# A GNN chain on one Trainium2 core: two norms without eigenvector pieces, the branch moved, three half blocks in the lead

## The chip, the cores and the metric

The kernel runs as one program on one core of a Trainium2 chip. Its time is the device time of one execution in microseconds (us). The engines are called as in the profile: PE (matmul, with PEld for its weight loads), DVE (vector), ACT (scalar), POOL (GpSimd) and SP, which here only issues DMAs. Each engine runs its own list of instructions in the order in which it was built; semaphores hold an instruction back until others have ended.

## What is computed

Four graph layers, each followed by `x = layernorm(x + layer(x))`, on x of 128 x 64 x 256 float32. The change touches layer 1, what leads from it into layer 2, and the eigenvectors of layer 3, which are worked out early, in pieces between other work.

```python
# layer 1: two matmuls, each with a norm over all 8192 rows
agg = jnp.einsum('nm,bmd->bnd', A_hat, features)
x = agg.reshape(-1, d)
h = jax.nn.relu(_batchnorm(x @ W1.T + b1, g1, be1))
out = h @ W2.T + b2
out = _batchnorm(out, g2, be2)
# layer 2, its edge scores:
e = jnp.einsum('behd,hd->beh', jax.nn.leaky_relu(Qs + Kt, 0.2), a)
# layer 3:
_, U = jnp.linalg.eigh(L_norm)
```

A batchnorm needs mean and variance of all rows before the first row can be scaled: at each of the two there is one point through which all work passes.

## The kernel before, in words

The 8192 rows are 64 tiles of 128 rows (`X`, kept on chip), taken four at a time as 16 blocks q (`NQ`).

**First pass** (loop at L1733). For each q, PE multiplies by the adjacency matrix (L1739) and by W1 (L1745, into `ps`); DVE takes the statistics of each result (`bn_stats` into `st1`, L1746); ACT copies it away (L1747). `pump(n)` puts about n us of eigenvector pieces, small DVE instructions and a few small matmuls, into the program at that place. `affine("n1", ...)` (L1709) turns the statistics into scale and shift: one `bn_aggr` for each of four groups (L1712), then a chain of small DVE steps with one square root on ACT (L1214), down to `n1sh` (L1722).

**Second pass** (loop at L1755). For each q ACT makes four pieces of `h` (L1758, in the order 2, 3, 0, 1), SP reloads X (L1759), PE multiplies by W2 (L1763, in the order 0, 1, 2, 3), DVE takes statistics (L1764) and copies the result to `Y` (L1765). `affine("n2", ...)` follows.

**The branch** (L1815). The fast eigenvector method leaves a flag `bad`; a general path stands behind a loop that runs 0 or 1 times by the value `again` (L1811). Every engine loads that value (TENSOR_LOAD), compares, jumps over the loop's body, and waits at the loop's exit until all engines have come there and all their earlier work has ended. The body has some 5,800 DVE instructions.

**Last pass** (`last_pass`, L1770) in 32 half blocks of two tiles. For half block h: ACT scales `Y` into `y` (L1778), PE transposes it (L1787), DVE adds it to X (L1234) and takes layernorm statistics (L1237, L1238). Every second half block `flush` works out the scale of four tiles: a DVE step (L1212), a square root on ACT (L1214), five DVE steps (L1215 to L1218, L1249), and ACT scales each tile (L1253). Each half block is two steps of a generator: transposes and add, then the rest.

**Scores of layer 2** (`scores`, L1910) run beside it, in 32 steps k of two tiles. A step transposes two normalised tiles (L1890, copied by DVE at L1892), maps them with a weight matrix (L1901; ACT copies at L1903 and L1904), and for c = 0 and 1 spreads them over edges (L1924, "l"), copies the result (ACT, L1931, four instructions), applies the leaky ReLU (DVE, L1932, four) and reduces with the vector a (PE, L1878). Four half blocks of the last pass come first; then every step k takes two more with it. The first l of a round waits for all four copies of the round before.

A scheduler places each instruction in its engine's list; the order in the source isn't the order in the list, except where `tc.issue_after` or `tc.keep_in_program_order` hold it.

Of the kernel before, what the change touches and what calls it, by code (L numbers as in the profile page):

```python
# [1 line left out]

# [5 lines left out]
F32 = mybir.dt.float32  # L8
I32 = mybir.dt.int32
AF = mybir.ActivationFunctionType  # L10
ALU = mybir.AluOpType
# [3 lines left out]
N = 64  # L15
# [1244 lines left out]
def tile_adj_resnorm(ctx: ExitStack, tc: tile.TileContext, I: dict, out: bass.AP, layers: int = 4):  # L1260
# [74 lines left out]
    def psum(rows, w):  # L1335
        return eps.tile([P, 512], F32, tag="eps", name="eps")[:rows, :w]
# [46 lines left out]
    def pump(n):  # L1383

        owed[0] += n
        body = nc.cur_bb.bb.instructions
        for i in reversed(body[seen[0] :]):
            if i.engine == mark[0].engine:
                mark[0] = i
                break  # L1390
        with tc.issue_after(mark[0]):
            while owed[0] > 0:
                owed[0] -= next(pieces, None) or 2.6
        seen[0] = len(body)
# [293 lines left out]
    own2 = lambda where, **k: own1(where, side="right", **k)  # L1688
    dram = keep1.enter_context(tc.tile_pool(name="l1d", bufs=1, space=bass.MemoryType.DRAM))
    lw, sm = own2(only1, name="l1w", bufs=1), own2(only1, name="l1s", bufs=2)  # L1690
    pp = own1(only1, name="l1p", bufs=7, space=PSUM)

    def lload(name, shape, src, eng=nc.sync):
        t = lw.tile(shape, F32, tag=name, name=name)
        eng.dma_start(t, src)
        return t

    NQ = NT // 4
    Y = [ly.tile([P, 2, 512], F32, tag=f"Y{q}", name="Y") for q in range(NQ)]
    w1 = lload("w1", [P, 2, 512], kio(I["W1T"]))  # L1700
    w2 = lload("w2", [P, 4, D], kio(I["W2T"]))
    vec1 = lload("vec1", [P, 3, 4], I["vec1"], s)
    vec2 = lload("vec2", [P, 3, 2], I["vec2"], s)
# [21 lines left out]
    def xq(q):  # L1725
        return X[:, q * 4 : q * 4 + 4, :]
# [5 lines left out]
    back = residual(NT // TG - 1, H, pp, "ps")  # L1732
    for q in range(NQ):  # L1733
        nc.sync.dma_start(xd[q], xq(q))
        at = sm.tile([P, 2, 512], F32, tag="at", name="at")
        for k in range(2):
            ps = pp.tile([P, 512], F32, tag="ps", name="ps")
            for j in range(4):
                te.matmul(ps[:, j * P : (j + 1) * P], X[:, q * 4 + j, k * P : (k + 1) * P], bdah,  # L1739
                          start=True, stop=True)  # L1740
            s.copy(at[:, k, :], ps)  # L1741
        for c in range(4):
            ps = pp.tile([P, 512], F32, tag="ps", name="ps")
            for k in range(2):
                te.matmul(ps, w1[:, k, c * P : (c + 1) * P], at[:, k, :], start=(k == 0), stop=(k == 1))  # L1745
            v.bn_stats(st1[:, c, q, :], ps)  # L1746
            s.copy(first(q, c), ps)  # L1747
        next(back, None)
        pump(4.5 if q < 8 else 6)
    zero = sm.tile([P, 1024], F32, tag="at", name="zero")  # L1750
    v.memset(zero, 0.0)
    for z in attn_d[: N * N, :].rearrange("(k p a) q -> k p (a q)", p=P, a=4):
        nc.sync.dma_start(z, zero)
    sc1, sh1 = affine("n1", st1, vec1, 4)
    for q in range(NQ):  # L1755
        h = sm.tile([P, 4, 512], F32, tag="h", name="h")
        for c in (2, 3, 0, 1):
            s.activation(h[:, c, :], first(q, c), AF.Relu, bias=sh1[:, c : c + 1], scale=sc1[:, c : c + 1])  # L1758
        nc.sync.dma_start(xq(q), xd[q])  # L1759
        for c in range(2):  # L1760
            ps = pp.tile([P, 512], F32, tag="ps", name="ps")
            for k in range(4):
                te.matmul(ps, w2[:, k, c * P : (c + 1) * P], h[:, k, :], start=(k == 0), stop=(k == 3))  # L1763
            v.bn_stats(st2[:, c, q, :], ps)  # L1764
            v.tensor_copy(Y[q][:, c, :], ps)  # L1765
        pump(5)
    sc2, sh2 = affine("n2", st2, vec2, 2)
    for _ in pieces:
        pass

    def last_pass():

        ln = Norm(nc, sy, X, 8, act=True)

        def normed(h):
            y = sy.tile([P, 2, 2 * P], F32, tag="y", name="y")
            for c in range(2):
                s.activation(y[:, c, :], Y[h // 2][:, c, h % 2 * 2 * P : (h % 2 + 1) * 2 * P], AF.Identity,  # L1778
                             bias=sh2[:, c : c + 1], scale=sc2[:, c : c + 1])
            return y  # L1780

        y = normed(0)
        for h in range(2 * NQ):
            ps = pp.tile([P, 512], F32, tag="m", name="m")
            for i in range(2):
                for c in range(2):
                    te.transpose(ps[:, i * D + c * P : i * D + (c + 1) * P], y[:, c, i * P : (i + 1) * P], ident)  # L1787
            ln.add(2 * h, ps, 2)
            yield
            if h % 2:  # L1790
                ln.flush()
            if h < 2 * NQ - 1:
                y = normed(h + 1)
            yield

    only1.close()
    beyond.close()
    own.close()


    def spread():
        for bd, m in ((bdu, U), (bdut, UT)):
            for b in range(2):
                r = slice(b * N, (b + 1) * N)
                v.tensor_copy(bd[r, r], m[r, :])

    with tc.tile_pool(name="eps3", bufs=1, space=PSUM) as eps:
        again = ek.tile([1, 1], I32, tag="again", name="again")
        ps = psum(1, 1)
        te.matmul(ps, fast.bad, ones[:N, 0:1], start=True, stop=True)  # L1810
        v.tensor_scalar(again, ps, 0.0, None, ALU.is_gt)  # L1811
        for bd in (bdu, bdut):
            v.memset(bd, 0.0)
        spread()
        with tc.For_i(0, nc.values_load(again[0:1, 0:1], min_val=0, max_val=1)):  # L1815
            with tc.tile_pool(name="gk2", bufs=1) as gk2, tc.tile_pool(name="gt2", bufs=1) as gt2, tc.tile_pool(
                name="gp2", bufs=1, space=PSUM
            ) as gp2:
                Eigh(tc, gk2, gt2, gp2, cst, ident, ones).from_leaves(*fast.state, U, UT)
            spread()  # L1820

    sy = own1(keep1, name="l1z", bufs=3)

# [3 lines left out]
    with ExitStack() as l2:  # L1827
# [67 lines left out]
        def maps(k, xT):  # L1895

            xq, xv = [], sx.tile([P, 2, D], F32, tag="xv", name="xv")
            for i in range(2):
                ps = pp.tile([P, 512], F32, tag="m", name="m")
                for c in range(2):  # L1900
                    te.matmul(ps, xT[:, i, c, :], wqv[:, c, :], start=(c == 0), stop=(c == 1))  # L1901
                xq.append(sx.tile([P, D], F32, tag="xq", name="xq", bufs=4))
                taken.append(s.copy(xq[i], ps[:, :D]))  # L1903
                s.copy(xv[:, i, :], ps[:, D:])  # L1904
            nc.sync.dma_start(xvd[k], xv)
            return xq

        def scores():


            K = NT // 2
            xT = transposed(0)
            xq, xT = maps(0, xT), transposed(1)


            four = [(b, i) for i in range(2) for b in range(2)]
            for k in range(K):
                xn = None
                for c in range(2):
                    xs, pl = {}, [pg.tile([P, 2, 512], F32, tag="l", name="l") for _ in range(2)]  # L1920
                    mms = []
                    for b, i in four:
                        r = slice(b * N, (b + 1) * N)
                        mms.append(te.matmul(pl[i][:, b, :], xq[i][r, c * P : (c + 1) * P], GG[r, :], start=True, stop=True))  # L1924
                    after(mms[0], taken)
                    del taken[:]
                    next(beside[0], None)
                    ready = []
                    for b, i in four:
                        x = xs[b, i] = sx.tile([P, E], F32, tag="xs", name="xs", bufs=6)  # L1930
                        taken.append(s.copy(x, pl[i][:, b, :]))  # L1931
                        ready.append(v.scalar_tensor_tensor(x, x, 0.2, x, ALU.mult, ALU.max))  # L1932
                    if late:
                        after(products(), mms[-1:], mybir.DependencyClass.NoSync)
                    late.append((k, c, xs, ready))
                    if c == 0 and k < K - 1:
                        xn = maps(k + 1, xT)
                    if c == 1 and k < K - 2:
                        xT = transposed(k + 2)
                    next(beside[0], None)  # L1940
                xq = xn
                if k == K - 1:
                    products()
                yield
# [91 lines left out]

        bank = None
        sc_, beside[0] = scores(), last_pass()
        run(*beside * 8)
        run(*[sc_] * (NQ - 2))  # L2040
        keep1.close()
        beside[0] = iter(())
        lw, sm = own1(valuing, name="l2w", bufs=1), own1(valuing, name="l2s", bufs=2)
        ln = Norm(nc, sm, X, 4, act=True)
        val = values()
        soft += [softmax(h, es[h]) for h in range(2)]
        run(*[sc_] * (HU - NQ + 2))
        for _ in range(3):
            run(sc_, soft[0], soft[0])
        run(soft[0], sc_)  # L2050
# [156 lines left out]
```

## Time and profile before

| | us |
|---|---|
| median of three runs | 2411.7 (2410.27 to 2413.79) |
| the profiled execution | 2413.07, span 2411.2 |

Busy time of PE by stretch of the span (a query over windows of the trace):

| stretch, us | what runs | PE busy | of |
|---|---|---|---|
| 1530 to 1570 | first pass | 39.83 | 40.00 |
| 1667 to 1676 | first norm | 2.09 | 9.00 |
| 1700 to 1740 | second pass | 40.00 | 40.00 |
| 1790 to 1803 | second norm, branch, first half blocks | 4.54 | 13.00 |
| 1803 to 1830 | half blocks, first scores | 22.16 | 27.00 |
| 1830 to 1900 | scores beside the last pass | 69.14 | 70.00 |

In lines of the timeline the columns are: start in us, length in us, engine, source line, operation, output<-input, shape, number of instructions merged, and in brackets how long the engine sat idle before, and what ended that. Lengths of PE matmuls are modelled; starts are measured.

### The profile page before, as it was taken

The page shows a single profiled execution, that of the slowest core. Times are in us where ns is not written, and L with a number is a line of the kernel's source. Part 1 is how long each engine was busy: PE and PEld are TensorE (multiplying, and loading weights), DVE is VectorE, ACT ScalarE, POOL GpSimd, SP SyncE. Part 2 cuts the span into 40 slices and gives each one's busy share as a digit, 9 for nine tenths or more (in the row PEclk, how much of TensorE's full clock was granted, in tenths as well). Part 3 has the DMA queues.
Part 4 walks back from the last instruction along what each step waited for, and adds up shares of the span by engine and source line. Part 5 has one row for each costly group of instructions (what it writes and reads, how often), then busy time and mean ns, then how long its engine had stood idle before and what let it go on. Part 6 is the DMA issues. An engine that isn't in the chain of part 4 may idle for free. (4 is left out here: it accounts for less than half of the span.)

```text
span 2411.2 us, 29498 instructions
## 1 busy us (share of the span) xinstructions
PE 2289.0 (95%) x9016; PEld 1226.7 (51%) x9016; DVE 1815.5 (75%) x8352; ACT 974.3 (40%) x1750; POOL 76.4 (3%) x115
## 2 busy tenths in 40 slices
PE   7999999999999999999999999998979999898897
PEld 5544654444565544665444644554434433246786
DVE  4666766677887888888888888686967877457577
ACT  2333322242333243332243322333437875456575
POOL 0000000000000000000000000000000000002231
PEclk9999999999999999999999999999989999999899
DMA  6001000000100010100001000012211000511622
GB/s 218 18 18 36 1 35 1 24 30 18 53 1 35 2 52 18 53 35 1 35 36 36 17 18 18 18 49 92 75 45 40 23 23 29 94 40 44 136 89 75
DMA packets 59861, 101.26 MB, mean 42 GB/s; under 512 B 5136, under 2 KB 40080, under 8 KB 59440
## 3 DMA queue, kind: packets, MB, share of 16 engines
q1 hardware_dynamic: 54624, 88.83, 11.6%
q0 software_dynamic: 3216, 10.21, 1.5%
q8 instruction: 72, 1.18, 0.2%
q14 instruction: 93, 0.76, 0.1%
q10 hardware_dynamic: 1856, 0.28, 0.1%
HBM read 67.84 MB, written 31.46 MB: 41 GB/s over the span
## 5 line engine op out<-in xcount | busy, mean ns | idle before, releaser
L1590 PE MATMUL pq<-H,wi 128*128 128x512 f32 (+1 forms) x2016 | 836.4, 547 | 6.1 <-DVE H L1619 4.0
L1596 ACT ACTIVATE gate<-pq,bl 128x512 f32<-128x512 f32 (+1 forms) x504 | 317.6, 635 | 791.0 <-PE pq L1594 642.3
L1590 PEld LDWEIGHTS pq<-H,wi 128*128 128x128 f32 x2016 | 371.9, 191 | 331.0 <-issue 256.7
L1594 PE MATMUL pq<-lh,wh 128*128 128x512 f32 (+1 forms) x1152 | 481.8, 534 | 16.0 <-DVE lh L1614 12.7
L1594 PEld LDWEIGHTS pq<-lh,wh 128*128 128x128 f32 x1152 | 213.1, 190 | 213.3 <-issue 128.3
L1932 DVE SCALAR_TENSOR_TENSOR xs<-xs 128x512 f32<-128x512 f32 x256 | 165.3, 682 | 63.6 <-ACT xs L1931 62.5
L1931 ACT COPY xs<-l 128x512 f32<-128x512 f32 x256 | 136.8, 587 | 74.8 <-PE l L1924 38.6
L1924 PE MATMUL l<-edge_s,xq 64*128 64x512 f32 x512 | 136.0, 629 | 17.5 <-ACT xs L1931 12.5
L1612 ACT ACTIVATE gate<-lc 128x512 f32<-128x512 f32 (+1 forms) x144 | 83.5, 580 | 166.6 <-DVE lc L1608 80.9
L1901 PE MATMUL m<-wqv,xT 128*128 128x512 f32 x256 | 123.0, 617 | 0.8 <-DVE xT L1892 0.8
L1763 PE MATMUL ps<-h,w 128*128 128x512 f32 x256 | 114.9, 608 | 6.9 <-ACT h L1758 6.9
L1745 PE MATMUL ps<-at,w 128*128 128x512 f32 x256 | 116.7, 607 | 3.8 <-ACT at L1741 3.2
L1253 ACT ACTIVATE X<-X,ln_sh,ln_rs 128x256 f32<-128x256 f32 x192 | 99.2, 590 | 19.5 <-DVE ln_sh L1249 13.7
L1237 DVE BATCH_NORM_STATS2 ln_st<-X 128x6 f32<-128x256 f32 x256 | 98.7, 415 | 2.3
L142 DVE COPY AQR<-eps 64x192 f32<-64x192 f32 (+1 forms) x125 | 35.0, 280 | 80.9 <-PE eps L148 80.8
L1901 PEld LDWEIGHTS m<-wqv,xT 128*128 128x128 f32 x256 | 46.0, 192 | 77.1 <-issue 62.5
L1763 PEld LDWEIGHTS ps<-h,w 128*128 128x128 f32 x256 | 49.1, 194 | 67.4 <-issue 57.5
L1924 PEld LDWEIGHTS l<-edge_s,xq 64*128 64x128 f32 x512 | 46.3, 189 | 69.8 <-issue 32.9
L1996 POOL DMA_DIRECT2D xr<-xv x32 | 17.6, 550 | 2007.2 <-DVE xs L1932 1791.2
L1610 DVE TENSOR_TENSOR gate<-gate 128x512 f32<-128x512 f32 (+1 forms) x72 | 43.4, 603 | 45.9 <-ACT gate L1596 45.3
L1745 PEld LDWEIGHTS ps<-at,w 128*128 128x128 f32 x256 | 47.2, 192 | 59.7 <-issue 46.8
L1878 PE MATMUL sc<-xs,az 128*32 128x512 f32 x512 | 68.2, 605 | 3.0 <-DVE xs L1932 3.0
(557 smaller groups left out, 3245.6 us busy)
## 6 DMA issues: line engine op xcount, KB each, us to landing
wi<-in_WihT_dram SPq DMA_DIRECT2D x16, 1024.0 KB, 4.9
wh<-in_WhhT_dram SPq DMA_DIRECT2D x12, 1024.0 KB, 6.9
X<-in_x_dram SPq DMA_DIRECT2D x16, 512.0 KB, 8.9
xd<-X SPq DMA_DIRECT2D x16, 512.0 KB, 2.7
X<-xd SPq DMA_DIRECT2D x16, 512.0 KB, 3.2
xv<-xv SPq DMA_DIRECT2D x32, 256.0 KB, 2.0
xr<-xv POOLq DMA_DIRECT2D x32, 256.0 KB, 3.0
M<-attn_d SPq DMA_DIRECT2D x16, 512.0 KB, 11.2
```

What stands on the lines that cost most here:

```text
L1237: nc.vector.bn_stats(st, self.X[:, k, :])
L1253: nc.scalar.activation(x, x, AF.Identity, bias=sh[:, k : k + 1], scale=rs[:, k : k + 1])
L1590: te.matmul(ps, wi[:, kk, o * P : (o + 1) * P], at(kk, k), start=(kk == 0), stop=(k == 0 and kk == 1))
L1594: te.matmul(ps, wh[:, kk, o * P : (o + 1) * P], hst[:, kk, :M], start=False, stop=(kk == 1))
L1596: s.activation(gates[gt][:, c, :M], ps, AF.Tanh if gt == 2 else AF.Sigmoid, bias=bl[:, p - 1, o : o + 1])
L1612: s.activation(g[2], cs, AF.Tanh)
L1745: te.matmul(ps, w1[:, k, c * P : (c + 1) * P], at[:, k, :], start=(k == 0), stop=(k == 1))
L1763: te.matmul(ps, w2[:, k, c * P : (c + 1) * P], h[:, k, :], start=(k == 0), stop=(k == 3))
L1901: te.matmul(ps, xT[:, i, c, :], wqv[:, c, :], start=(c == 0), stop=(c == 1))
L1924: mms.append(te.matmul(pl[i][:, b, :], xq[i][r, c * P : (c + 1) * P], GG[r, :], start=True, stop=True))
L1931: taken.append(s.copy(x, pl[i][:, b, :]))
L1932: ready.append(v.scalar_tensor_tensor(x, x, 0.2, x, ALU.mult, ALU.max))
```

## The change

First pass: no pieces are pumped at q = 15 and fewer at q = 14 (3 instead of 6), more at q = 8 to 13 (6.5 instead of 6), and `pump(5)` stands behind the first norm. W1, the input pieces `at` and the block of zeros move to a pool `la` that is closed after the pass. The zeros and the cleared matrices `bdu`, `bdut` are written by POOL instead of DVE. Second pass: PE takes the four pieces of h in the order in which ACT makes them. The flag is worked out after q = 14 (`find_bad`), and the branch stands between the last matmuls (q = 15) and the last statistics; the last two copies to `Y` stand after the second norm. Last pass: three half blocks lead instead of four, the third between the first maps and transposes of the scores; the first half block is flushed alone; ACT's order is held for the first four. The scores run 15 steps beside the last pass instead of 14.

```diff
-        pump(4.5 if q < 8 else 6)
-    zero = sm.tile([P, 1024], F32, tag="at", name="zero")
-    v.memset(zero, 0.0)
+        if q < NQ - 1:
+            pump(4.5 if q < 8 else 6.5 if q < NQ - 2 else 3)
+    zero = la.tile([P, 1024], F32, tag="at", name="zero")
+    nc.gpsimd.memset(zero, 0.0)
...
     sc1, sh1 = affine("n1", st1, vec1, 4)
+    pass1.close()
+    def find_bad():
+        again = ek.tile([1, 1], I32, tag="again", name="again")
+        ps = psum(1, 1)
+        te.matmul(ps, fast.bad, ones[:N, 0:1], start=True, stop=True)
+        v.tensor_scalar(again, ps, 0.0, None, ALU.is_gt)
+        for bd in (bdu, bdut):
+            nc.gpsimd.memset(bd, 0.0)
+        spread()
+        return again
+    def general_path():
+        with tc.For_i(0, nc.values_load(again[0:1, 0:1], min_val=0, max_val=1)):
+            with tc.tile_pool(name="gk2", bufs=1) as gk2, tc.tile_pool(name="gt2", bufs=1) as gt2:
+                Eigh(tc, gk2, gt2, eps, cst, ident, ones).from_leaves(*fast.state, U, UT)
+            spread()
+            v.memset(st2[:, :, NQ - 1, :], 0.0)
+    pump(5)
...
-            for k in range(4):
-                te.matmul(ps, w2[:, k, c * P : (c + 1) * P], h[:, k, :], start=(k == 0), stop=(k == 3))
-            v.bn_stats(st2[:, c, q, :], ps)
-            v.tensor_copy(Y[q][:, c, :], ps)
-        pump(5)
+            for k in (2, 3, 0, 1):
+                te.matmul(ys[c], w2[:, k, c * P : (c + 1) * P], h[:, k, :], start=(k == 2), stop=(k == 1))
+        if q == NQ - 1:
+            general_path()
+        for c in range(2):
+            v.bn_stats(st2[:, c, q, :], ys[c])
+            if q < NQ - 1:
+                v.tensor_copy(Y[q][:, c, :], ys[c])
+        if q < NQ - 2:
+            pump(5)
+        elif q == NQ - 2:
+            for _ in pieces:
+                pass
+            again = find_bad()
     sc2, sh2 = affine("n2", st2, vec2, 2)
+    for c in range(2):
+        tc.keep_in_program_order(v.tensor_copy(Y[NQ - 1][:, c, :], ys[c]))
...
-            if h % 2:
-                ln.flush()
-            if h < 2 * NQ - 1:
-                y = normed(h + 1)
+            with in_order(s, h < 4):
+                if h < 2 * NQ - 1:
+                    y = normed(h + 1)
+            with in_order(s, h < 4):
+                if h % 2 or not h:
+                    ln.flush()
...
-            xq, xT = maps(0, xT), transposed(1)
+            xq = maps(0, xT)
+            next(beside[0])
+            xT = transposed(1)
+            next(beside[0])
...
-        run(*beside * 8)
-        run(*[sc_] * (NQ - 2))
+        run(*beside * 4)
+        run(*[sc_] * (NQ - 1))
```

What the scheduler makes of it can be read from the lists of the two built programs. PE's list is the same up to the end of the second pass, but for the order within a group of four matmuls and for the flag's small matmul, which goes in ahead of q = 15. In one score step k the lists of ACT and DVE stand as follows (PE's is the same in both: l, sc, map, yT, l, sc, xT, yT, each standing for four matmuls). The names: yT and xT are transposes of y and X, xT' the copy by DVE; xs and lr the copy and the leaky ReLU behind an l (a for c = 0, b for c = 1); xq, xv the two copies behind one half of a map; add, st, ag the add and statistics of a half block; t1 to t6 and sq the seven small steps of a flush, X its scalings; a number is a count.

```
ACT before: xs2(a) y2 xs2(a) | xq xv xq xv | y2 xs2(b) sq xs2(b) X4
ACT after:  y2 | xs2(a) sq xs2(a) | xq xv X3 xq xv X | y2 xs4(b)
DVE before: xT' lr2(b) | add st2 lr(a) lr3(a) | add st2 t1 lr2(b) t2 t3 t4 t5 t6
DVE after:  xT' lr2(b) | add st2 lr(a) lr(a) t1 t2 t3 t4 t5 lr2(a) t6 | add st2 lr2(b)
```

After the change the flush belongs to the half block whose transposes stand ahead of the first l of a step; before, to the other one. From the first y on, ACT's list begins so (0a: first round of step 0):

```
ACT before: y13 sq y sq X8 | xq xv xq xv | xs4(0a) y2 | xq xv xq xv | y2 xs2(0b) sq xs2(0b) X4 | xs2(1a) y2 xs2(1a) | xq xv xq xv
ACT after:  y4 sq X2 y2 sq X2 | xq xv xq xv | y2 xs4(0a) | xq xv xq xv | y2 sq y2 X4 xs4(0b) | y4 xs2(1a) y2 xs2(1a) | xq xv sq X xq xv X3
```

More of the change, by code (lines that the diff above doesn't have):

```diff
@@ L1 @@
-from contextlib import ExitStack
+from contextlib import ExitStack, contextmanager, nullcontext
 import concourse.bass as bass
@@ L1690, in tile_adj_resnorm @@
     lw, sm = own2(only1, name="l1w", bufs=1), own2(only1, name="l1s", bufs=2)
+    pass1 = ExitStack()
+    la = own2(pass1, name="l1a", bufs=2)
     pp = own1(only1, name="l1p", bufs=7, space=PSUM)
@@ L1699, in tile_adj_resnorm @@
     Y = [ly.tile([P, 2, 512], F32, tag=f"Y{q}", name="Y") for q in range(NQ)]
-    w1 = lload("w1", [P, 2, 512], kio(I["W1T"]))
+    w1 = la.tile([P, 2, 512], F32, tag="w1", name="w1", bufs=1)
+    nc.sync.dma_start(w1, kio(I["W1T"]))
     w2 = lload("w2", [P, 4, D], kio(I["W2T"]))
@@ L1734, in tile_adj_resnorm @@
         nc.sync.dma_start(xd[q], xq(q))
-        at = sm.tile([P, 2, 512], F32, tag="at", name="at")
+        at = la.tile([P, 2, 512], F32, tag="at", name="at")
         for k in range(2):
@@ L1754, in tile_adj_resnorm, with spread @@
     sc1, sh1 = affine("n1", st1, vec1, 4)
+    pass1.close()
+    def spread():
+        for bd, m in ((bdu, U), (bdut, UT)):
+            for b in range(2):
+                r = slice(b * N, (b + 1) * N)
+                v.tensor_copy(bd[r, r], m[r, :])
+    def find_bad():
[14 more added lines that the diff above has]
+    pump(5)
     for q in range(NQ):
@@ L1759, in tile_adj_resnorm, with in_order @@
         nc.sync.dma_start(xq(q), xd[q])
+        ys = []
         for c in range(2):
-            ps = pp.tile([P, 512], F32, tag="ps", name="ps")
-            for k in range(4):
-                te.matmul(ps, w2[:, k, c * P : (c + 1) * P], h[:, k, :], start=(k == 0), stop=(k == 3))
-            v.bn_stats(st2[:, c, q, :], ps)
-            v.tensor_copy(Y[q][:, c, :], ps)
-        pump(5)
-    sc2, sh2 = affine("n2", st2, vec2, 2)
-    for _ in pieces:
-        pass
+            ys.append(pp.tile([P, 512], F32, tag="ps", name="ps"))
+            for k in (2, 3, 0, 1):
[12 more added lines that the diff above has]
+            again = find_bad()
+    sc2, sh2 = affine("n2", st2, vec2, 2)
+    for c in range(2):
+        tc.keep_in_program_order(v.tensor_copy(Y[NQ - 1][:, c, :], ys[c]))
+    @contextmanager
+    def in_order(eng, on):
+        last = next((i for i in reversed(nc.cur_bb.bb.instructions) if i.engine == eng.engine), None) if on else None
+        with tc.issue_after(last) if last is not None else nullcontext():
+            yield
     def last_pass():
@@ L1798, in tile_adj_resnorm @@
     own.close()
[L1801 to L1820, printed above, removed]
     sy = own1(keep1, name="l1z", bufs=3)
@@ L2046, in tile_adj_resnorm @@
         soft += [softmax(h, es[h]) for h in range(2)]
-        run(*[sc_] * (HU - NQ + 2))
+        run(*[sc_] * (HU - NQ + 1))
         for _ in range(3):
```

## The prediction

> **What bounds the kernel now.** PE does: 2289.0 of 2411.2 us busy on the page. So only stretches where PE starves can pay, and a longer round trip elsewhere can cost. I read the page, then the windows, then the timeline of the two norms, then one score step. First norm, second norm with branch:
>
> ```profile
> 1671.83 0.15 DVE L1722 TENSOR_TENSOR n1sh<-n1t,vec 128x4 f32<-128x4 f32 x1
> 1672.01 1.52 ACT L1758 ACTIVATE h<-X,n1sh,n1sc 128x512 f32<-128x512 f32 x2 [2.04 <-DVE n1sh L1722]
> 1674.29 18.16 PE L1763 MATMUL ps<-h,w 128*128 128x512 f32 x35 [6.91 <-ACT h L1758]
> ...
> 1793.91 0.16 DVE L1722 TENSOR_TENSOR n2sh<-n2t,vec 128x2 f32<-128x2 f32 x1
> 1797.99 6.50 ACT L1778 ACTIVATE y<-Y,n2sh,n2sc 128x256 f32<-128x256 f32 x13 [5.30 <-issue]
> 1798.65 3.37 PE L1787 MATMUL m<-ident,y 128*128 128x128 f32 x12 [8.09 <-ACT y L1778]
> ```
>
> PE starves 6.91 us at the first norm: it begins when the third piece of h is there, 2.28 us after ACT began. At the second it starves 8.09 us, and 3.9 of them lie between a ready scale (1794.07) and the first y: ACT jumps over the general path. The chain has that jump:
>
> ```profile
> 1793.41 3.58 issue
> ```
>
> One score step beside the last pass (DVE, then ACT, then PE):
>
> ```profile
> 1959.25 0.17 DVE L1215 RECIPROCAL is_r<-is_s 128x4 f32<-128x4 f32 x1
> 1960.06 0.16 DVE L1249 SCALAR_TENSOR_TENSOR ln_sh<-ln_mv,ln_rs 128x4 f32<-128x4 f32 x1
> 1960.14 0.68 DVE L1892 COPY xT<-m 128x512 f32<-128x512 f32 x1
> 1960.74 1.28 DVE L1932 SCALAR_TENSOR_TENSOR xs<-xs 128x512 f32<-128x512 f32 x2
> 1961.94 0.68 DVE L1234 TENSOR_TENSOR X<-m,X 128x512 f32<-128x512 f32 x1
> 1963.41 0.66 DVE L1932 SCALAR_TENSOR_TENSOR xs<-xs 128x512 f32<-128x512 f32 x1
> 1964.08 1.86 DVE L1932 SCALAR_TENSOR_TENSOR xs<-xs 128x512 f32<-128x512 f32 x3
> ...
> 1958.36 0.22 ACT L1214 ACTIVATE is_s<-is_t 128x4 f32<-128x4 f32 x1
> 1960.26 2.07 ACT L1253 ACTIVATE X<-X,ln_sh,ln_rs 128x256 f32<-128x256 f32 x4
> ...
> 1960.35 1.99 PE L1924 MATMUL l<-edge_s,xq 64*128 64x512 f32 x8
> 1967.43 1.99 PE L1924 MATMUL l<-edge_s,xq 64*128 64x512 f32 x8
> 1969.34 1.07 PE L1878 MATMUL sc<-xs,az 128*32 128x512 f32 x8
> 1970.34 0.66 PE L1890 MATMUL m<-ident,X 128*128 128x128 f32 x4
> 1971.55 1.99 PE L1924 MATMUL l<-edge_s,xq 64*128 64x512 f32 x8 [0.56 <-ACT xs L1931]
> ```
>
> A step lasts 11.20 us (1960.35 to 1971.55), nearly all PE's own work, with DVE and ACT at some four fifths (58.89 and 58.23 of 70 us from 1830). The add at 1961.94 waits behind the transposed copy and two leaky ReLUs, 1.59 us after l began. That is harmless here because the flush comes half a step later.
>
> [...]the first y waited behind the branch (5.30 us). [...]after 6.91 us of idleness weight loads came every 0.85 us up to 1680.28, then every 0.43. [...]3.58 us on ACT, about 3.0 us on DVE (its branch records stop at 1794.95 and go on at 1797.9).
>
> **The change, part by part.**
>
> *First norm.* Without pieces the last statistics (0.70) start with PE's end, 1667.45; the last aggregate ends at 1668.8. From there the second norm, which had no pieces, shows 1.78 us (1792.29 to 1794.07), so ACT begins at about 1670.65 instead of 1672.01. PE takes the first piece of h, ready 0.77 us later, not the third: start near 1671.45 instead of 1674.29, 2.8 us gained. Half clock follows a gap of 4.1 us or doesn't; its cost before was 3.0 us (half of 1674.29 to 1680.28). I count no gain, 1.3 at the best end, because a 3.03 us gap ahead of the first pass (PE idle until 1519.67) also cost half clock. The skipped pieces go into the second pass; DVE waits there for PE (5.50 us before 1680.90), which covers them.
>
> *Zeros and clears on POOL.* Idle until 1817 but for its loads at the start; DVE loses a 0.91 us memset. If POOL were as slow as 5 us for the zeros, SP's writes would wait, then the X reloads behind them on its queue; these are needed 120 us later. Nothing either way. W1 loaded behind W2 on SP: both landed 40 us before use (issued 1472.4, 1472.9; landing 3.8 and 4.8 us). Nothing.
>
> *Branch.* The flag is ready about 5.4 us before PE's end (the second last pair of statistics and copy ran 1783.61 to 1784.90; PE ended 1790.40)[...]. If that cover goes, up to 3.6 us come back. New: the last two statistics now stand behind the loop's exit, which waits for PE's last matmul. Exit about 0.6 us after PE's end (five more waits of 0.05 on DVE, and the jump), two statistics 1.24, two aggregates 1.13, then 1.78: y at 4.8 us after PE's end instead of 7.59. Gain 2.8 (bounds 1.5 and 3.3). The flag's matmul inside PE's stream costs 0.3.
>
> *Ramp, from the first y.* Before: X scaled from 8.55, maps 11.15, l(0a) 17.33, l(0b) 23.80, l(1a) 27.93, l(2a) 39.13. After, by the lists: the first half block alone is added at 2.09, statistics and seven small steps done by 6.0, so maps at 8.65, l(0a) 14.85, l(0b) 21.8. The lead is 2.0 to 2.5 us here. But l(1a) needs the copies 0b, and ACT now has sq, y2 and X4 ahead of these: y2 to 22.9, sq, small steps to 24.1, X4 to 26.1, xs4 to 28.3. l(1a) at 28.4: lead gone. In step 1 sq sits between the xq, and its DVE step waits behind four leaky ReLUs (until 34.4): l(1b) 36.8 instead of 35.0, l(2a) about 41.6, 2.5 us late. Bounds 1 and 4.
>
> *The ring in each later step.* After the change the lists close a ring through one step: add of the half block, statistics, lr(a) twice, t1, sq (ACT can't pass it), t2 to t5, the other two lr(a) whose xs stood behind sq, t6, three X ahead of the second xq, that xq, l(b), sc, xT, its copy, two lr(b), and the next add. From the rows, start to start: add to first lr 1.47 (1961.94 to 1963.41); to the second 0.67; to t1 0.60 (half of the pair's 1.20); t1 to sq 0.20, sq to t2 0.24 (second norm: 1792.29, 1792.49, 1792.73); t2 to t5 0.60; to lr 0.08; two lr 1.20; t6 to X 0.20; three X 1.48; xq to l 0.43 (1967.00 to 1967.43); l to sc 1.91; sc to xT 1.00; xT to its copy 0.70; copy to lr 0.60; two lr 1.20. Sum 12.6 us a step, against PE's 11.2. ACT's own list closes at the same l: xs, y2 and the rest end 4.28 us after the second xq, as PE's path does (4.27). Step 2 still gains from the ramp (11.9), steps 3 to 13 take 12.6, step 14 up to the next l 13.6 instead of 11.91. So l of step 15 comes 41.6 + 11.9 + 138.6 + 13.6 = 205.7 us after the first y; before, 185.5 (1983.46 - 1797.99). Loss 20.2. Bounds per step 12.2 and 13.1 (lr at 0.65 instead of 0.60, other waits), that is -5 and +6. Behind that PE's list is the same, and the later stall for the softmax (2.56 us before an sc) is a chain of its own that moves with it.
>
> *Sum.* -2.8 - 2.8 + 0.3 + 20.2 = +14.9. Against this execution 2413.07 + 14.9 = 2428.0; it lies 1.4 above the median of the runs, so 2426.6 there.
>
> **Rivals.**
>
> *The ring doesn't close (faster).* If the terms come out 1.4 us shorter, as when the add isn't behind the copy and two lr (1.6 us of the ring), steps stay at 11.2 and step 1 doesn't lose either: the ramp's 2.0 us stay, 2411.7 - 5.3 - 2.0 = 2404. It decides where a step falls under 11.3. For it: the change meant more lead, and DVE is at 84%. Against: every link is an order within one engine or a semaphore, and each duration is measured.
>
> *It closes by half (same).* Steps at 11.6 (the add at once, X still ahead of xq): 13 x 0.4 + 2.5 - 5.3 = +2.4, 2414.
>
> *The branch isn't hidden (slower still).* [...]3.6 us come back: 2430.
>
> **How the numbers follow.** Forecast 0.83, not hidden 0.07, by half 0.04, not closed 0.06. A change under 0.2%, 4.8 us, can't be told from none. Slower 0.89 (the forecast reaches down to 2418 with all good ends, still above 2416.5), same 0.04, faster 0.07. The range 2415 to 2437: 12.2 to 13.1 us a step, both ends of ramp and norms, and the fourth case.
>
> **What would show it.** PE's gap at the first norm near 4.1 us; y 4.8 us after the last W2 matmul with no long issue on ACT before it; first maps 8.7 us after the first y. Then a step of 12.6 us from l(a) to l(a), ACT idle some 2 us in front of sq with DVE as the releaser, PE idle ahead of l(b) and l(a). A step of 11.2 would make the prediction wrong, and the time 2404 to 2408; one over 13.2 would too.

## The result

The changed kernel takes 2432.01 us (median of four runs, 2430.75 to 2433.33) against 2411.55 for the kernel before (four runs): ratio 1.0082, 95% interval 1.0066 to 1.0098. It is slower by 20.5 us. The forecast was 2426.6 with a range of 2415 to 2437: the measured time lies in the range and on the right side, 5.4 us above the forecast. The profiled execution took 2431.46, its span 2429.7.

Cut at the points that the prediction used, the two profiled executions compare as follows (starts from the timelines; an end of PE is the next start less the idle time in brackets; only the second pass of the kernel before is taken to end at 1790.40, as in the prediction, since the flag's two small matmuls follow there until 1790.56).

| stretch | before, us | after, us | difference | forecast |
|---|---|---|---|---|
| span's start to layer 1's first adjacency matmul | 1514.70 | 1515.48 | +0.78 | none |
| to the first W1 matmul | 4.97 | 7.85 | +2.88 | 0 |
| first pass from there to PE's end | 147.71 | 148.09 | +0.38 | 0 |
| PE idle at the first norm | 6.91 | 4.11 | -2.80 | -2.8 |
| second pass to PE's end | 116.11 | 116.62 | +0.51 | +0.3 |
| PE's end to the first y | 7.59 | 5.14 | -2.45 | -2.8 |
| first y to the l of score step 15 | 185.47 | 205.98 | +20.51 | +20.2 |
| from there to the span's end | 427.74 | 426.43 | -1.31 | 0 |
| sum | 2411.2 | 2429.7 | +18.5 | +14.9 |

The first and the last row hold the same work of PE in both kernels. Their differences, and the 2 us by which these two executions lie off their medians, are of the size of the scatter: over the twelve traces of this case the first row runs from 1513.85 to 1516.62, and the last is 425.8 and 427.6 in two of the experiments below (four half blocks in the lead, with W1 late and with W1 early), which have the same instructions there.

**The two norms.** Timeline of the changed kernel, the first norm, then the second with the branch ahead of it:

```profile
1671.46 0.70 DVE L1749 BATCH_NORM_STATS2 st<-ps 128x6 f32<-128x512 f32 x1 [0.40 <-PE ps L1748]
1674.47 0.16 DVE L1725 TENSOR_TENSOR n1sh<-n1t,vec 128x4 f32<-128x4 f32 x1
1674.67 1.52 ACT L1790 ACTIVATE h<-X,n1sh,n1sc 128x512 f32<-128x512 f32 x2 [1.44 <-DVE n1sh L1725]
1675.53 8.88 PE L1796 MATMUL ps<-h,w 128*128 128x512 f32 x14 [4.11 <-ACT h L1790]
...
1786.21 0.14 DVE L1773 TENSOR_SCALAR again<-eps 1x1 int32<-1x1 f32 x1
1793.08 1.29 DVE L1800 BATCH_NORM_STATS2 st<-ps 128x6 f32<-128x512 f32 x2 [6.73 <-PEq L1780]
...
1797.09 0.16 DVE L1725 TENSOR_TENSOR n2sh<-n2t,vec 128x2 f32<-128x2 f32 x1
1797.29 2.07 ACT L1827 ACTIVATE y<-Y,n2sh,n2sc 128x256 f32<-128x256 f32 x4 [1.41 <-DVE n2sh L1725]
1797.94 2.38 PE L1836 MATMUL m<-ident,y 128*128 128x128 f32 x8 [5.79 <-ACT y L1827]
```

The last statistics start as PE ends, and PE begins again 0.86 us after ACT began its first piece of h: the gap is 4.11. At the second norm the flag is known at 1786.35, 5.8 us before PE's end (1792.15); the last statistics wait for PE at the loop's exit (releaser PEq L1780), and y follows its scale at once, where before 3.9 us lay between the two. Both edits do what they were meant to.

**W1's load.** Timeline of the changed kernel around the first pass's start:

```profile
1519.04 0.69 DVE L1619 TENSOR_TENSOR H<-gate 128x512 f32<-128x512 f32 x1 [0.75 <-ACT gate L1612]
1519.79 0.37 SPq L1703 DMA_DIRECT2D w<-in_W1T_dram  x1
1519.82 1.07 ACT L1744 COPY at<-ps 128x512 f32<-128x512 f32 x2 [0.81 <-DVE H L1619]
1523.33 2.90 PE L1748 MATMUL ps<-at,w 128*128 128x512 f32 x3 [5.91 <-DMA w<-in_W1T_dram]
```

and SP's waits, by total time (waiting line, releaser, us in total, times, longest):

```profile
SPq L1703 <- DVE H L1619: 93.0, 1, 93.0
```

The load stood on SP for 93 us and went out 0.06 us after layer 0's very last write to H. Before, it was issued at 1472.4. The matmul now waits for the transfer instead of for ACT's copy.

**The score steps.** One step of the changed kernel, the main lines of DVE, ACT and PE as one timeline:

```profile
1943.94 0.16 DVE L1212 TENSOR_SCALAR is_t<-ln_mv 128x4 f32<-128x4 f32 x1
1944.14 0.20 ACT L1214 ACTIVATE is_s<-is_t 128x4 f32<-128x4 f32 x1 [1.95 <-DVE is_t L1212]
...
1945.07 1.26 DVE L1964 SCALAR_TENSOR_TENSOR xs<-xs 128x512 f32<-128x512 f32 x2
1946.25 0.15 DVE L1249 SCALAR_TENSOR_TENSOR ln_sh<-ln_mv,ln_rs 128x4 f32<-128x4 f32 x1
1946.44 1.58 ACT L1253 ACTIVATE X<-X,ln_sh,ln_rs 128x256 f32<-128x256 f32 x3 [0.59 <-DVE ln_sh L1249]
1947.93 0.35 ACT L1932 COPY xq<-m 128x256 f32<-128x256 f32 x1
1948.33 1.99 PE L1956 MATMUL l<-edge_s,xq 64*128 64x512 f32 x8 [1.34 <-ACT xq L1932]
1950.25 1.07 PE L1907 MATMUL sc<-xs,az 128*32 128x512 f32 x8
1951.24 0.66 PE L1919 MATMUL m<-ident,X 128*128 128x128 f32 x4
1951.33 1.07 ACT L1963 COPY xs<-l 128x512 f32<-128x512 f32 x2 [0.35 <-PE sc L1907]
1951.74 0.60 PE L1836 MATMUL m<-ident,y 128*128 128x128 f32 x4
1951.94 0.69 DVE L1921 COPY xT<-m 128x512 f32<-128x512 f32 x1
1952.46 1.99 PE L1956 MATMUL l<-edge_s,xq 64*128 64x512 f32 x8
1952.55 1.28 DVE L1964 SCALAR_TENSOR_TENSOR xs<-xs 128x512 f32<-128x512 f32 x2
1953.75 0.68 DVE L1234 TENSOR_TENSOR X<-m,X 128x512 f32<-128x512 f32 x1
1955.21 0.66 DVE L1964 SCALAR_TENSOR_TENSOR xs<-xs 128x512 f32<-128x512 f32 x1
1956.46 0.16 DVE L1212 TENSOR_SCALAR is_t<-ln_mv 128x4 f32<-128x4 f32 x1
1956.66 0.21 ACT L1214 ACTIVATE is_s<-is_t 128x4 f32<-128x4 f32 x1 [1.95 <-DVE is_t L1212]
```

Follow it down: square root, the last two leaky ReLUs, shift, three scalings, xq, l(b), sc, xT, its copy, two leaky ReLUs, add, and the next square root: 1944.14 to 1956.66 is 12.52 us. PE is idle 1.34 us in front of l(b), about as much as the step is longer than before (12.52 against 11.20). From 1830 to 1980 it is busy for 132.03 of 150 us, before for 147.66, with the same work per step. The page has the same in its groups (busy and mean ns, then idle time ahead and what ended most of it):

```profile
L1964 DVE SCALAR_TENSOR_TENSOR xs<-xs 128x512 f32<-128x512 f32 x256 | 165.2, 680 | 88.7 <-ACT xs L1963 88.2
L1956 PE MATMUL l<-edge_s,xq 64*128 64x512 f32 x512 | 135.7, 624 | 36.2 <-ACT xq L1932 19.9
L1253 ACT ACTIVATE X<-X,ln_sh,ln_rs 128x256 f32<-128x256 f32 x192 | 101.0, 591 | 30.7 <-DVE ln_sh L1249 24.9
```

The idle time ahead of l was 17.5 us before, the leaky ReLU's 63.6, that of X 19.5: all three wait longer for one another, and no engine is full (of the 150 us DVE is busy for 114.62 and ACT for 113.42).

### The profile page after: what moved, and what is told of

The parts are those of the page before. It is cut to its first block, busy times and chain, and to the rows that moved or that the text cites. A ratio compares the mean times of both kernels' runs of the same rounds, so it can differ in the third digit from the quotient of the medians.

```text
span 2429.7 us, 29499 instructions
## 1 busy us (share of the span) xinstructions
PE 2289.1 (94%) x9016; PEld 1225.0 (50%) x9016; DVE 1817.8 (75%) x8355; ACT 974.1 (40%) x1751; POOL 77.4 (3%) x118
## 3 DMA queue, kind: packets, MB, share of 16 engines
q8 instruction: 72, 1.18, 0.2%
## 5 line engine op out<-in xcount | busy, mean ns | idle before, releaser
L1550 PE MATMUL ps<-wg,h 128*128 128x256 f32 x256 | 65.4, 394 | 5.9 <-DVE h L1541 5.5
```

## The experiments

The theory after the result: the ring costs the 20 us, alone; W1's load costs 2.9; the two norms bring some 5. Medians below are those of each run; "before" ran beside every group, at 2411.6 to 2412.3.

**Is it the last pass and its lead alone?** First the changed kernel with these parts as before:

```diff
-            with in_order(s, h < 4):
-                if h < 2 * NQ - 1:
-                    y = normed(h + 1)
-            with in_order(s, h < 4):
-                if h % 2 or not h:
-                    ln.flush()
+            if h % 2:
+                ln.flush()
+            if h < 2 * NQ - 1:
+                y = normed(h + 1)
...
-            xq = maps(0, xT)
-            next(beside[0])
-            xT = transposed(1)
-            next(beside[0])
+            xq, xT = maps(0, xT), transposed(1)
...
-        run(*beside * 4)
-        run(*[sc_] * (NQ - 1))
+        run(*beside * 8)
+        run(*[sc_] * (NQ - 2))
...
-        run(*[sc_] * (HU - NQ + 1))
+        run(*[sc_] * (HU - NQ + 2))
```

> The changed kernel with the last pass and the lead of the kernel before (four half blocks ahead, a flush after every odd half block, no order held on ACT); norms, branch, W1's new place stay. Ring theory (the loss is the step's order alone): steps of 11.2 us again, the l of step 15 comes 185.5 us after the first y instead of 206.0, so the time falls by 20.5 to 2411.5. Rival (the loss sits in the early parts: W1's load, norms, branch): steps 11.2 but the time stays above 2420.

Measured: 2410.79, ratio to before 0.9996 (0.9987 to 1.0005). Steps of 11.20, l of step 15 at 186.06. Then the opposite: the kernel before with only these lines changed.

> The kernel before with nothing but the new last pass and lead (three half blocks, first one flushed alone, ACT's order held for four). Ring theory: steps of 12.5 us, l of step 15 at 206.0 us after the first y, 2411.5 + 20.5 = 2432. Rival (the loss needs the other parts of the change): under 2422.

Measured: 2433.84, ratio 1.0095 (1.0077 to 1.0113); steps of 12.52 and 12.53, l of step 15 at 205.16. Either way 21 to 22 us go with these lines, and nothing else in the change is needed for it.

**The number of leading half blocks, or the place of the flush?** Three still lead, but the flush moves by one half block:

```diff
-                if h % 2 or not h:
+                if h < 3 or h % 2 == 0 or h == 2 * NQ - 1:
```

The lists of one step (names as in the change's section), changed kernel and this one:

```
ACT after: y2 | xs2(a) sq xs2(a) | xq xv X3 xq xv X | y2 xs4(b)
ACT here:  xs2(a) y2 xs2(a) | xq xv xq xv | y2 xs2(b) sq xs2(b) X4
```

> The changed kernel, three half blocks ahead as in the change, but flushed after half blocks 0, 1, 2 and then every even one, so that the flush falls into the other half of a score step. Ring theory (what counts is the half of the step in which square root and scalings of X stand on ACT, not how many half blocks lead): steps of 11.2 us; the beginning is slower than with four (eight y stand ahead of the copies of l(0b) and l(1a), l(1a) near 29.9 us after the first y instead of 27.9), so 2413 to 2414. Rival (a lead of three is too short for the score steps, whatever the order): steps stay at 12.5 us and the time at 2432.

Measured: 2414.65, ratio 1.0009 (1.0003 to 1.0016). Steps of 11.20; l(1a) at 29.53. The rival is out: three leading half blocks bear a step of 11.20 well. Only the last step beside the last pass, step 14, takes 13.08; before, with no half block beside it any more, it took 11.91; here the single flush of half block 31 stands in front of a second xq. This was not expected, and the time is 0.65 above the 2413 to 2414 of the expectation.

**Does the step grow with work that is put into the ring?** A copy that nothing reads, once a step, behind the statistics that the flush waits for. It leaves ACT's and PE's lists as they were in the steady steps of both kernels; in the changed one a reciprocal (t5) also moves behind two leaky ReLUs, which are inside the ring too.

```diff
             ln.add(2 * h, ps, 2)
+            if h % 2:
+                v.tensor_copy(pad, X[:, 2 * h + 1, :256])
             yield
```

> The changed kernel with one more DVE copy of 128x256 elements, which nothing reads, right behind the statistics of every second half block, so inside the closed ring: once a score step. Ring theory: each step grows by the whole length of the copy, about 0.35 us (half of the 128x512 copy's 0.69), from 12.52 to 12.85 or so, the time by 4 to 5 us. Rival (ACT's or PE's amount of work sets the step): DVE is busy for some three quarters of the stretch, so an added 0.35 us is absorbed and the step stays at 12.52.

Timeline of this kernel:

```profile
1953.80 0.68 DVE L1234 TENSOR_TENSOR X<-m,X 128x512 f32<-128x512 f32 x1
...
1955.27 0.26 DVE L1839 COPY pad<-X 128x256 f32<-128x256 f32 x1
...
1956.71 0.17 DVE L1212 TENSOR_SCALAR is_t<-ln_mv 128x4 f32<-128x4 f32 x1
...
1961.13 1.99 PE L1958 MATMUL l<-edge_s,xq 64*128 64x512 f32 x8 [1.57 <-ACT xq L1934]
```

The copy took 0.26 us, not 0.35. From add to t1 it is 2.91 us now, against 2.71 (1953.75 to 1956.46) above: 0.20 more. The step is 12.75, 0.23 longer, PE's gap at l(b) likewise 1.57 instead of 1.34. Here added work on an engine with a quarter of its time free lengthened a step by about what it added: 0.23 us for 0.26, and 3.1 us up to the l of step 15 (209.09 after the first y). The execution's time, 2432.39, doesn't show these 3.1 us: its first y came 2.2 us earlier than the changed kernel's (1795.12 against 1797.29), in stretches that the copy doesn't touch. So the steps carry this reading, and the 4 to 5 us expected of the time are missed.

> The kernel before with the additional copy of e4_pad_after (a DVE copy of 128x256 elements behind the statistics of every second half block). Theory (PE sets the step there, DVE and ACT have slack, no ring is closed): steps stay at 11.20 us, where the changed kernel went from 12.52 to 12.75. Rival (DVE is nearly the bound there too): steps grow by up to 0.23 us to 11.43.

Measured in the kernel before: steps of 11.20 and 11.21, unchanged. There the same copy is free. (One execution each; this one took 2413.28.)

**A period worked out ahead of the run.** ACT's order of the source is held for all half blocks (`in_order(s, True)` at both places), so that X stands behind both xq:

```
ACT here: xs4(a) | xq xv xq xv | y2 sq xs(b) X4 xs3(b) | y2
```

> The changed kernel with ACT's order of the source held for all half blocks, not four: in each step ACT runs xs(a) four times, both xq and xv, y, the square root, one xs(b), X four times, three xs(b). The scalings stand behind both xq, but in front of three copies of l(b). Theory (a step is as long as the longest ring that the lists close, added up link by link): l(a) to xq to l(b) 7.6, then y and square root 1.4 behind that xq, six small steps 1.1, one leaky ReLU, an add and another leaky ReLU 1.9, matmuls sc and xT 1.6, next l(a): 14.1 us a step (13.3 by ACT's list alone: X 2.1 and three xs 1.6 behind the small steps), the time near 2453. Rival (it is enough that X no longer stands in front of xq): steps of 11.2 us, 2412.

Measured: steps of 13.57, 2446.95 (one execution). Timeline of this kernel:

```profile
1954.98 1.99 PE L1956 MATMUL l<-edge_s,xq 64*128 64x512 f32 x8 [0.46 <-ACT xq L1932]
1955.08 1.10 ACT L1827 ACTIVATE y<-Y,n2sh,n2sc 128x256 f32<-128x256 f32 x2
1956.08 0.20 ACT L1214 ACTIVATE is_s<-is_t 128x4 f32<-128x4 f32 x1
...
1957.32 2.08 ACT L1253 ACTIVATE X<-X,ln_sh,ln_rs 128x256 f32<-128x256 f32 x4 [0.57 <-DVE ln_sh L1249]
...
1959.31 1.52 ACT L1963 COPY xs<-l 128x512 f32<-128x512 f32 x3
1960.88 1.99 PE L1956 MATMUL l<-edge_s,xq 64*128 64x512 f32 x8 [1.75 <-ACT xs L1963]
```

l(a) to l(b) takes 7.66 (forecast 7.6), l(b) to l(a) 5.90. The rival falls: to take X away from xq isn't enough. But the 14.1 us expected for a step is missed. I had counted two leaky ReLUs of l(b) as l(a)'s, and so a way through sc and xT that isn't there: the l that ends the step waits for ACT's three copies, 0.05 us after the last of them. The ring by ACT's list, expected at 13.3, is the one that closes.

**W1.** The kernel of the first experiment, with W1's tile again in the pool that stays open:

```diff
-    w1 = la.tile([P, 2, 512], F32, tag="w1", name="w1", bufs=1)
-    nc.sync.dma_start(w1, kio(I["W1T"]))
+    w1 = lload("w1", [P, 2, 512], kio(I["W1T"]))
```

> As e1_four_lead, and W1 back in the pool that stays open to the end of the layer, as in the kernel before. Theory (W1's load in the new pool had to wait until layer 0's last write to the space below it, and the first W1 matmul waits 5.91 us instead of 3.03): the load is issued near 1472 us again, PE's gap ahead of the first W1 matmul is 3.0 us, the time 2.9 below e1_four_lead: 2407.9, ratio to before 0.9983. Rival (the first matmul waits for the copies by ACT anyway, or the saved time returns as idleness at the first norm): no change against e1_four_lead, 2410.8.

Timeline of this kernel:

```profile
1472.57 0.38 SPq L1697 DMA_DIRECT2D w<-in_W1T_dram  x1
...
1519.81 10.08 PE L1747 MATMUL ps<-at,w 128*128 128x512 f32 x16 [3.03 <-ACT at L1743]
```

Issue and gap are back (5.89 without it). The time is 2408.84, ratio 0.9982 (0.9975 to 0.9989). Against the first experiment that is 2.0 less by the medians and 3.4 by the two ratios, where 2.9 were expected; the intervals leave all of these open. So the 2.9 is what the trace shows of the gap, and the time agrees in sign.

**The first norm alone.** The changed kernel with `pump(4.5 if q < 8 else 6)` at every q, no `pump(5)` behind the norm, and W2's order 0, 1, 2, 3.

> The changed kernel with the first norm as before: eigenvector pieces pumped at q = 14 and 15, W2's matmuls in the order 0, 1, 2, 3. Theory (that part alone gains 2.8 us, and 0.5 of half clock): PE's gap at the first norm 6.9 us instead of 4.1, 2432.0 + 2.8 to 3.3 = 2435. Rival (the time gained there is lost again in the second pass, where the skipped pieces go): 2432.

```profile
1677.82 12.71 PE L1794 MATMUL ps<-h,w 128*128 128x512 f32 x22 [6.88 <-ACT h L1788]
```

In this kernel's timeline PE's gap is 6.88 again. From PE's end of the first pass to its end of the second: 123.47 us (1670.94 to 1794.41), in the changed kernel 120.73 (1671.42 to 1792.15). So 2.7 us are gained by the trace. This hides two smaller effects in the second pass that nearly cancel. PE ran at half clock (weight loads came every 0.85 us instead of every 0.43) for 6.11 us from its start here, and for 5.28 in the changed kernel, where the granted clock of that stretch was 0.50; half of the difference, 0.4 by estimate, is part of the 2.7. And the changed kernel waits for an eigenvector piece in the second pass:

```profile
1756.88 0.24 PE L183 MATMUL eps<-ident,delta 64*64 64x64 f32 x1 [0.36 <-DVE delta L124]
```

At this matmul neither this kernel nor the kernel before is idle. So the rival, that the second pass takes the gain back, holds for some 0.4 of 2.8 us. The time, 2434.16, ratio 1.0091 (1.0076 to 1.0107), is 2.2 above the changed kernel's, a little under the expected 2.8.

**Can the lead be had without the ring?** The flush on even half blocks, W1 early, and ACT's order held for two half blocks (`h < 2`).

> As e3_even_flush, with W1 early and ACT's order held for the first two half blocks instead of four, so that ACT's list comes into its steady order before l(0b): y, a square root and single X between the first copies, no eight y in a row. Theory: the early start of the first maps (8.6 us after the first y) is kept, l(1a) near 26 us after the first y instead of 27.9 before, all steps 11.2, the last with the lead perhaps 13.1 as in e3_even_flush; l of step 15 at 184.5 after the first y; 2406.5. Rival (PE's own list sets the beginning, the lead can't be kept): l(1a) at 28 or later, 2408 to 2411.

Measured: 2408.49, ratio 0.9983 (0.9976 to 0.9989). l(0a) comes at 15.00 (before 17.33), but l(1a) at 27.50, not 26. PE's list in this kernel:

```profile
1809.78 1.12 PE L1955 MATMUL l<-edge_s,xq 64*128 64x512 f32 x2
1810.84 0.66 PE L1918 MATMUL m<-ident,X 128*128 128x128 f32 x4
1811.42 1.98 PE L1955 MATMUL l<-edge_s,xq 64*128 64x512 f32 x6
1813.34 0.66 PE L1835 MATMUL m<-ident,y 128*128 128x128 f32 x4
1813.83 3.82 PE L1929 MATMUL m<-wqv,xT 128*128 128x512 f32 x8
1817.49 0.60 PE L1835 MATMUL m<-ident,y 128*128 128x128 f32 x4
1818.15 1.99 PE L1955 MATMUL l<-edge_s,xq 64*128 64x512 f32 x8
```

No line from l(0a) (1809.78) to l(1a) (1822.28) has an idle time in brackets: from the first l on PE is the bound. It takes 12.50 us from l(0a) to l(1a), before 10.60. Of these 1.9 us, 0.6 are four transposes that were done ahead of l(0a) before. 1.1 are l(0a) itself: the transposes stand in its middle here, and the two parts take 1.06 (1809.78 to 1810.84) and 1.92 us, where the whole took 1.92 before. Of 2.3 us of lead 0.4 stay. The last step beside the last pass takes 13.08, 1.2 more than before (11.91).

That last flush was then held on ACT behind the copies of the next step:

```diff
+            last = h == 2 * NQ - 1
+            if last:
+                yield
+                yield
-            with in_order(s, h < 2):
-                if h < 3 or h % 2 == 0 or h == 2 * NQ - 1:
+            with in_order(s, h < 2 or last):
+                if h < 3 or h % 2 == 0 or last:
                     ln.flush()
```

> As e6_even_flush_short_hold, but the single flush of the last half block is held on ACT behind the copies of the next score step, so that its square root and scalings no longer stand in front of a second xq. Theory (that flush cost 1.9 us once, 13.08 instead of 11.20, as the ring does in every step of the changed kernel): the last step with the lead takes about 11.2 to 11.9, l of step 15 comes 185.1 us after the first y or earlier, 2407.3. Rival (the flush stalls whatever stands behind it, wherever it is): the loss moves into the next step and l of step 16 comes no earlier than in e6_even_flush_short_hold (206.8 after the first y).

Measured: that step takes 11.90 instead of 13.08, as it did before (11.91): the flush cost 1.2 us there, not 1.9. The l of step 15 comes at 184.49 instead of 186.26 (0.5 of this was there at l(0a) already), and the l that the expectation calls that of step 16 (counted as elsewhere here, it opens step 17) at 205.05 instead of 206.82. Nothing returns in the next steps. 2407.34, ratio 0.9983 (0.9975 to 0.9990). These three versions (this one, the one before it, and four leading half blocks with W1 early) are faster than the kernel before by 0.17 to 0.18%; between them no run here tells.

## Why the prediction was right, and where it was off

- **The ring** (12.6 us a step): measured 12.52 from step 3 to 13. Link by link from the timeline above and its neighbours: add to first leaky ReLU 1.46 (forecast 1.47), to t1 0.67 and 0.58, to the square root 0.20, t2 0.23, t5 0.61, to the leaky ReLU 0.09, two of them 1.18, to X 0.19, to xq 1.49, to l(b) 0.40, to sc 1.92, to xT 0.99, its copy 0.70, leaky ReLU 0.61, two of them and the add 1.20: 12.52. The signs named ahead are there: ACT idle 1.95 in front of the square root with DVE as releaser, PE idle ahead of l(b). One is hardly there: ahead of l(a) PE is idle for 0.12 us in the steady steps (1952.34 to 1952.46 above). The prediction had ACT's list and PE's end this half of the step within 0.01 us of each other. In the trace ACT's last copy ends 0.06 us before l(a); it had itself waited 0.35 us for PE's sc.
- **The ramp**: maps 8.64 us after the first y (8.65), l(0a) 15.06 (14.85), l(0b) 23.17 (21.8), l(1a) 29.56 (28.4), l(1b) 38.03 (36.8), l(2a) 42.68 (41.6). From l(0b) on it is 1.1 to 1.4 late: the xq ahead of l(0b) waits for PE's maps of step 1, which run 3.60 us from 1816.40 on, and for this the prediction left too little time. Step 2 took 12.29 (11.9), steps 3 to 13 0.8 less in all, step 14 13.23 (13.6): 205.98 against 205.7 in sum. So the sum is nearer than its terms.
- **"W1 loaded behind W2 on SP ... Nothing"** is the step that failed: +2.88 us, where the prediction put nothing. The working looked at SP's queue and at when the load had landed before. It didn't ask who had used the new pool's space last. The wait for H's last write (93 us on SP) and the run with W1 back in its old pool show it.
- **First norm**: 2.80, as worked out; alone 2.7 by the trace of the run that undoes it. **Branch**: hidden, as said. The jump over the general path, on ACT from 1793.37 to 1796.98 before (3.6 us) and on DVE from 1794.94 to 1797.94 (3.0), now lies beside q = 15: from 1787.25 to 1789.96 (2.7) and from 1787.41 to 1790.55 (3.1). DVE began behind the loop's exit 0.93 us after PE's end instead of 0.6, so 2.45 instead of 2.8. **Second pass**: +0.51 instead of +0.3. Three terms make up most of this: the flag's matmuls, 0.31 (the last sixteen of W2's matmuls and the flag take 7.18 us from start to start, W2's alone 6.87 before), as forecast; a wait for one eigenvector piece, 0.44 (the matmul at 1756.88 starts 0.96 us after the one ahead of it, before 0.52); and a half clock that ended 0.7 us sooner (5.28 after the start, before 5.99), worth half of that, -0.35. The remaining 0.1 stays open. The prediction had the skipped pieces covered by DVE's waits for PE; for this one piece that failed. In the **first pass** the half clock lasted 4.14 us instead of 3.51, which is 0.3 of the +0.38.
- **The rivals**: that the ring doesn't close, or by half, is refuted by 12.52; that the branch isn't hidden, by y, which starts 0.20 us after the last step of its scale does.
- The sum was 3.6 short of the profiled execution's 18.5: 2.9 for W1, 0.35 for the exit, 0.2 for the second pass, 0.3 for the ring with its ramp; the first and last rows and the first pass nearly cancel (-0.15). The remaining 2 us to the medians' 20.5 are where the two profiled executions lie (1.5 above the median of before, 0.55 below that of after).

## What to carry to other kernels

When a loop runs over several engines, add up the longest ring that their lists close through one round. Here the sum was 12.6 us and a step took 12.52, with DVE busy for 114.62 of 150 us and ACT for 113.42. Moving a small operation by half a round can open or close such a ring (the flush moved by one half block: 11.20 instead of 12.52), so compare the lists of a round before asking whether a longer lead helps. A tile put into another pool also took over the history of that space here: ask who used it last, for the load stood on SP for 93 us until that write had ended.

## What the runs showed of the hardware

- PE ran at half clock after each of the gaps listed in the next point, down to 3.03 us. Ahead of the first W1 matmul of the kernel before (a gap of 3.03), the granted clock was 1.00 from 1517.00 to 1519.67 and 0.51 in the 3.51 us that followed, with weight loads every 0.85 us instead of every 0.43. In two of the experiments (four half blocks in the lead with W1 early; the flush on even half blocks with the short hold) loads came every 0.85 us after a gap of 3.03 or 3.04 too. After the gap of 4.11 at the first norm the changed kernel's granted clock was 0.50 from 1675.53 to 1680.82.
- In these traces a longer gap didn't always go with a longer half clock. From the first matmul until loads came every 0.43 us it took 3.46 to 6.05 us after gaps of 3.03 and 3.04 (three traces), 3.26 to 5.28 after 4.11 (five), 3.40 to 4.18 after 5.82 to 5.91 (four), 5.99 and 6.11 after 6.91 and 6.88. The same gap of 4.11 gave 5.28 us in the changed kernel and 3.26 with four leading half blocks and W1 early. So the gap shortened from 6.91 to 4.11 us gained its own 2.80, and after one and the same gap the half clock alone moved a stretch by up to 1.0 us between traces, after 3.03 by up to 1.3 (estimates: half of 5.28 - 3.26 and of 6.05 - 3.46).
- A DVE copy of 128x256 float32 inside SBUF took 0.26 us, where a 128x512 copy out of PSUM took 0.69 (L1921 in the changed kernel's step). That is less than the half of 0.69 that was expected.
